# First Fourier layer as 32x32 matmuls over one 32-row operand, with transfer queues in program order

## The chip, the cores and the metric

The kernel runs on one NeuronCore of one Trainium2 chip. The core has a matrix engine (TensorE, PE in the profile; its weight loads are listed apart as PEld), a vector engine (VectorE, DVE), a scalar engine (ScalarE, ACT), GpSimd (POOL) and SyncE (SP). Here SP and POOL do hardly anything but issue transfers. All transfers share the core's 16 DMA engines. Matmul results go to PSUM, an accumulator memory that DVE and ACT read out. The metric is the device time of one execution in microseconds (us); lower is better. All arithmetic is in fp32, and every fp32 matmul appears in the profile as two instructions (two passes), each with its own weight load.

## The reference, cut to what matters

Eight images of 8 channels and 256x256 pixels pass through two blocks. The first, `conv_preact`, is a small Fourier neural operator with a residual; the second is a 3x3 dilation with a residual.

```python
x = x + L0(_gn(x))        # _gn: normalised over 2 channels per group
x = x + L1(_gn(x))        # L1: maximum over a 3x3 window, border -2

def L0(x):                # G = 4 groups, 2 channels each
    h = gconv1x1(concat(x, grid_row, grid_col), fc0_w, fc0_b)   # 10 channels per group
    for i in range(4):
        h1 = spectral_conv(h, sp_w1[i], sp_w2[i])  # rfft2, 12 + 12 rows x 12 columns, irfft2
        h2 = gconv1x1(h, w_w[i], w_b[i])
        h = h1 + h2
        if i < 3: h = gswish(h, betas[i])          # h * sigmoid(softplus(beta) * h) / 1.1
    h = gswish(gconv1x1(h, fc1_w, fc1_b), betas[3])   # 10 -> 128 per group
    return gconv1x1(h, fc2_w, fc2_b)                  # 128 -> 2 per group
```

The change concerns the first pass of the loop (i = 0, "layer 0" below). There h is a linear map of x and of the pixel's coordinates, and both versions take h2 from x directly, with fc0 and w_w multiplied into one matrix.

## The kernel before, in words

**State.** The hidden state of one image lies in one SBUF tile `h`, 128 partitions by 11 chunks (`NCH`) by 4 by 512. Each block of 32 partitions holds 3 row blocks of 10 channels (30 rows used), and the two inner dimensions hold pairs of image rows, so that a chunk carries at most 24 rows of every channel.

**A layer.** For each layer `l` of 0 to 3, `spectrum_h` and `mix` (for layer 0 `spectrum_x` and `mix`, from the image itself) make the layer's output spectrum on PE and DVE. Their result is `fz`, 32 rows by 10 channels by 4 groups by 32 columns; column 24 holds a constant term and column 25 a term linear in the pixel's column. `rows_of` turns the column transform of `fz` into the tile `zt` with matmuls (L397 or L402). Then `layer` walks over the 11 chunks:

- `burst(c)` (L442) forms the chunk's new state in two PSUM tiles. First come 16 matmuls for the 1x1 convolution: K=32, M=32, N=512 from `h` (L452) in layers 1 to 3, and K=6, M=32, N=512 from `x` (L449) in layer 0, where `h` holds only 6 rows of `x` in each block. Then 8 matmuls, K=32, M=128, N=256, add the row transform `zt` times the table `binv` of waves (L455). ACT reads the two PSUM tiles back into `h` with the activation (L461, or L463 in layer 3).
- `turn(c-1)` transposes the previous chunk (16 matmuls, L424; two copies out by L194), and `transform(c-2)` takes its forward transform (L437, copy L438). Both are for the next layer, and layer 3 has neither.
- In layer 3 `stored[c]` (L465) writes the chunk to DRAM from SP.

**The head.** `head(b)` is a generator of 128 steps over the stored state of image b: `load_state` (L580, 256 KB on SP), `first` (8 matmuls L588, two activations L590) and, every second step, `second` (16 matmuls L610, a DVE add L615 into the tile `y`, which was loaded from `x` at L603). It runs inside the layers of image b+1. The generators yield costs, and the main loop (L705 to L718) hands out head steps between the chunks: in layers 0 to 2 two, one, one steps per chunk (`CHUNK`), in layer 3 two per chunk (`LAST`). `dilate(b)` runs behind the head, a piece after each such step, with its loads and stores on POOL (L646, L674).

**The next image's start.** `start(b+1)` loads spectral weights (`load_sw`, L342, 400 KB) and the image (`load_x`, L73, two times 1 MB, on SP), takes statistics on DVE (L227, L199) and small PE matmuls (L202, L210), and goes on to the spectrum and `mix`. It is handed out as side work of layer 3: `room += SIDE` (4.2) per chunk, less what each piece yields. By these costs the load belongs to chunk 0, the first four L227 to chunk 1, L202 and L210 to chunk 3, and the load of the third spectral weight (L360) to chunk 9, after that chunk's `stored`.

**Order.** All PSUM tiles of 2 banks share one tag with 4 buffers (`ps_z`, L57). The main loop stands in `tc.manual_schedule(engines={PE, DVE, ACT})`: those three run in the order written, and the framework's scheduler chooses the order of the instructions on SP and POOL. For layer 0 all 44 loads of `x` rows (`read_x`, L467, 48 KB each) are written ahead of the chunk loop; the rows can be overwritten once `stored[c]` of the image before has been read out.

Of the kernel before, what the change touches and what calls it, by code (L numbers as in the profile page):

```python
# [10 lines left out]
F32 = mybir.dt.float32  # L11
# [9 lines left out]
G = 4  # L21
# [19 lines left out]
LAST = (2,)  # L41
SIDE = 4.2
# [3 lines left out]
def fno_dilate_kernel(ctx: ExitStack, tc: tile.TileContext, a: dict, out: bass.AP):  # L46
    nc = tc.nc
    mm = nc.tensor.matmul
    PE, DVE, ACT = mybir.EngineType.PE, mybir.EngineType.DVE, mybir.EngineType.Activation
# [41 lines left out]
    wt = load("wt", (128, 4, G, 32))  # L91
    eh0 = load("eh0", (128, 3, 2, 32), nc.sync)
# [14 lines left out]
    h = const.tile([128, NCH, NQ, PIX], F32, tag="h", name="h")  # L107
    yin = const.tile([128, DR + 2, HW + 2], F32, tag="yin", name="yin")
# [12 lines left out]
    def softplus(t, n, name):  # L121
        e = const.tile([128, n], F32, tag=f"{name}_e", name=f"{name}_e")
# [5 lines left out]
        sp = const.tile([128, n], F32, tag=f"{name}_sp", name=f"{name}_sp")  # L128
# [3 lines left out]
        rs = const.tile([128, n], F32, tag=f"{name}_rs", name=f"{name}_rs")  # L132
# [6 lines left out]
    sp_p, rs_p = softplus(beta_p, 4, "bp")  # L139
    sp_a, rs_a = softplus(beta_a, 4 * G, "ba")  # L140
# [9 lines left out]
    wc = const.tile([128, 32], F32, tag="wc", name="wc")  # L150
# [13 lines left out]
    cv = const.tile([3, WID, G], F32, tag="cv", name="cv")  # L164
# [180 lines left out]
    def mix(b, l, out_):  # L345
# [28 lines left out]
        if l == 0:  # L374
# [6 lines left out]
                p[0:1, 240 : 240 + WID * G].rearrange("p (o g) -> p o g", o=WID), ALU.add)  # L381
        if l < 2:
            nc.vector.tensor_copy(fz[0:32, :, :, 25], cz[:, 4 if l == 0 else 3])
# [31 lines left out]

    def layer(b, l, out_, stored, side):
# [25 lines left out]
        def burst(c):  # L442
            pair = [ps_z(f"p_z_{b}_{l}_{c}_{i}") for i in range(2)]
            for f in range(NQ):
                for q in range(NQ):
                    o = pair[q // 2][part(f), q % 2, :]
                    if l == 0:
                        k = slice(32 * q, 32 * q + 6)
                        mm(o, wcn[k, :], h[k, c, f, :], start=True, stop=False)  # L449
                    else:  # L450
                        g = f if group_in_f else q
                        mm(o, wt[part(q), l, g, :], h[part(q), c, f, :], start=True, stop=False)  # L452
            for s in range(2):
                for q in range(NQ):
                    mm(pair[q // 2][:, q % 2, HW * s : HW * (s + 1)],  # L455
                       zt[part(q), 2 * c + s].rearrange("p f o -> p (f o)"), binv[part(q), :],
                       start=False, stop=s == 1)
# [9 lines left out]
        def read_x(c):  # L467
            for g in range(G):
                nc.sync.dma_start(
                    h[32 * g : 32 * g + 6, c].rearrange("p f w -> p (f w)"), a["xp"][b, c, g])  # L470

        if l == 0:
            for c in range(NCH):
                read_x(c)
            wcn = sb.tile([128, 32], F32, tag="wcn", bufs=1, name=f"wcn_{b}")
            nc.vector.tensor_scalar(wcn, wc, out_["mr"][:, 1:2], None, ALU.mult)
        room = 0.0
        yield ()
        for c in range(NCH):
            burst(c)  # L480
# [24 lines left out]
    def layers(b, stored, d, then):  # L505

        for l in range(4):  # L510
            if l > 0:
                yield from spectrum_h(b, l, d)
                yield from mix(b, l, d)
            yield from rows_of(b, l)
            yield from layer(b, l, d, stored, then if l == 3 else iter(()))
        yield from then


    spare = h.rearrange("p c f w -> p (c f w)")
# [48 lines left out]
    def head(b, stored, stats):  # L568
        hs, acts, box = {}, {}, {}
# [5 lines left out]
        def load_state(k):  # L575

            if k < NQ * NCH:
                j, c = k // NCH, k % NCH
# [301 lines left out]
```

## Time and profile before

| | us |
|---|---|
| median of 3 runs (4303.44 to 4309.84) | 4309.13 |
| the profiled execution, its own time | 4309.43 |
| its span, first to last instruction | 4307.7 |

| engine | busy us | share of the span | instructions |
|---|---|---|---|
| PE | 4089.1 | 95% | 52330 |
| PEld | 1925.6 | 45% | 52330 |
| ACT | 2772.9 | 64% | 2886 |
| DVE | 2297.3 | 53% | 3424 |
| POOL | 117.0 | 3% | 202 |

The mean granted PE clock is 0.982. The queues moved 344.65 MB, 80 GB/s over the span. In a timeline a row begins with the start and the duration in us; several instructions of one kind are merged (x16), and square brackets hold the idle time of that engine before it and what released it. Because matmuls are pipelined and their ends modelled, the time that a group of matmuls takes is read from its start to the start of the next group, not from its busy time.

### The profile page before, as it was taken

To read this page: it belongs to the slowest core of one execution; us is meant where nothing else is said; L and a number is where in the kernel's file an instruction comes from. 1 tells how busy PE (TensorE), PEld (TensorE's weight loads), DVE (VectorE), ACT (ScalarE), POOL (GpSimd) and SP (SyncE) were. 2 spreads that over 40 slices of the span, in tenths; PEclk is the share of its full clock that TensorE was granted. 3 is DMA by queue.
4 is the path that set the end of the run, shared out by engine and by line. 5 is a ranking of instruction groups with operands and counts; after the bars stand their busy time and mean duration, and the time that the engine had idled before them with its cause. 6 is when DMAs were issued, how large, how long until landed. Compare 5 with 4: busy or idle time off the path is not lost. (4 is left out here: it accounts for less than half of the span.)

```text
span 4307.7 us, 115455 instructions
## 1 busy us (share of the span) xinstructions
PE 4089.1 (95%) x52330; PEld 1925.6 (45%) x52330; DVE 2297.3 (53%) x3424; ACT 2772.9 (64%) x2886; POOL 117.0 (3%) x202
## 2 busy tenths in 40 slices
PE   5877999999999999999999999999999999999997
PEld 3544454444443444434444354444454444444222
DVE  4444544555655555655556555655655555654433
ACT  3435656766667666576666756667666766567887
POOL 1000000000000000000000000000000000000000
PEclk8988999999999999999999999999999999999999
DMA  2014101332114221242112511134111332114321
GB/s 78 13 40 151 53 28 43 135 103 62 55 53 161 87 62 52 75 171 58 52 59 81 182 42 53 50 104 159 55 45 53 136 120 62 48 57 147 109 60 46
DMA packets 113682, 344.65 MB, mean 80 GB/s; under 512 B 15611, under 2 KB 18107, under 8 KB 97768
## 3 DMA queue, kind: packets, MB, share of 16 engines
q1 hardware_dynamic: 95000, 276.18, 20.3%
q0 software_dynamic: 18192, 61.08, 4.3%
q8 instruction: 411, 6.73, 0.7%
q14 instruction: 79, 0.65, 0.1%
HBM read 213.21 MB, written 123.74 MB: 78 GB/s over the span
## 5 line engine op out<-in xcount | busy, mean ns | idle before, releaser
L590 ACT ACTIVATE act<-p_fc 128x1024 f32<-128x1024 f32 x2048 | 1968.9, 1025 | 1202.4 <-PE p_fc L588 1200.6
L588 PE MATMUL p_fc<-hs,c_w 32*128 32x512 f32 x8192 | 1191.6, 633 | 15.3 <-DVE turned L194 8.6
L610 PE MATMUL p_fc<-act,c_w 128*32 128x512 f32 x8192 | 986.7, 597 | 38.9 <-ACT act L590 25.6
L194 DVE COPY turned<-p_t 128x1024 f32<-128x1024 f32 x495 | 584.6, 1219 | 707.7 <-PE p_t L424 707.0
L588 PEld LDWEIGHTS p_fc<-hs,c_w 32*128 32x128 f32 x8192 | 383.6, 183 | 622.8 <-issue 240.9
L461 ACT ACTIVATE h<-p_z 128x1024 f32<-128x1024 f32 x528 | 512.9, 1023 | 117.4 <-PE p_z L455 116.7
L424 PE MATMUL p_t<-ident,h 128*128 128x128 f32 x4224 | 525.8, 278 | 0.0
L615 DVE TENSOR_TENSOR y<-p_fc,y 128x512 f32<-128x512 f32 x392 | 270.7, 690 | 474.9 <-PE p_fc L610 473.0
L610 PEld LDWEIGHTS p_fc<-act,c_w 128*32 128x32 f32 x8192 | 229.9, 109 | 647.4 <-issue 333.0
L424 PEld LDWEIGHTS p_t<-ident,h 128*128 128x128 f32 x4224 | 463.3, 142 | 98.5 <-ACT act L590 64.7
L455 PE MATMUL p_z<-c_binv,zt 32*128 32x256 f32 x5632 | 408.6, 404 | 1.0 <-ACT zt L192 1.0
L455 PEld LDWEIGHTS p_z<-c_binv,zt 32*128 32x128 f32 x5632 | 258.3, 185 | 304.4 <-issue 292.7
L452 PE MATMUL p_z<-h,c_wt 32*32 32x512 f32 x8448 | 317.0, 601 | 0.0
L437 PE MATMUL p_d<-turned,c_fw 128*32 128x240 f32 x4224 | 268.1, 371 | 4.1 <-ACT act L590 2.1
L194 DVE COPY zt<-p_g 128x264 f32<-128x264 f32 x300 | 159.0, 626 | 139.8 <-PE p_g L397 75.0
L463 ACT ACTIVATE h<-p_z,c_bias 128x1024 f32<-128x1024 f32 x176 | 186.6, 1111 | 26.4 <-PE p_z L455 25.9
L355 DVE TENSOR_REDUCE S<-turned 128x80 f32<-128x800 f32 x192 | 188.8, 983 | 5.0
L352 DVE TENSOR_TENSOR turned<-t,B 128x800 f32<-128x800 f32 x192 | 188.4, 981 | 0.5 <-DMA t<-in_spw 0.4
L452 PEld LDWEIGHTS p_z<-h,c_wt 32*32 32x32 f32 x8448 | 72.3, 103 | 190.1 <-ACT act L590 85.7
L437 PEld LDWEIGHTS p_d<-turned,c_fw 128*32 128x32 f32 x4224 | 109.6, 108 | 100.4 <-issue 39.1
L194 DVE COPY turned<-p_at 88x1024 f32<-88x1024 f32 x90 | 101.7, 1155 | 73.8 <-PE p_at L313 73.8
L438 DVE COPY zt<-p_d 128x240 f32<-128x240 f32 x264 | 105.5, 400 | 51.1 <-PE p_d L437 51.1
(170 smaller groups left out, 2023.8 us busy)
## 6 DMA issues: line engine op xcount, KB each, us to landing
stored<-h SPq DMA_DIRECT2D x88, 1024.0 KB
hs<-stored SPq DMA_DIRECT2D x352, 256.0 KB
t<-in_spw SPq DMA_DIRECT2D x96, 400.0 KB
yin<-y_rows POOLq DMA_DIRECT2D x56, 512.0 KB, 4.7
h<-in_xp SPq DMA_DIRECT2D x352, 48.0 KB
turned<-in_x SPq DMA_DIRECT2D x16, 1024.0 KB
y<-in_x SPq DMA_DIRECT2D x56, 256.0 KB
y_rows<-y POOLq DMA_DIRECT2D x56, 256.0 KB, 2.4
```

The source lines that it names most:

```text
L194: nc.vector.tensor_copy(dst, src)
L352: nc.vector.tensor_tensor(pr, sw[k], bt[:, k2, k].unsqueeze(2).to_broadcast([128, G, 2 * WID, WID]), ALU.mult)
L355: nc.vector.tensor_reduce(s[k2][:, k].rearrange("p g s o -> p (g s o)"), pr.rearrange("p g m i -> p (g m) i"), AX.X, ALU.add,)
L424: nc.tensor.transpose(t[:, i // 4, 128 * (i % 4) : 128 * (i % 4 + 1)], h[:, c, i // 2, 256 * (i % 2) + 128 * v : 256 * (i % 2) + 128 * (v ...
L437: mm(p[part(g), :240], fw[:, v, :], m[:, :, :, : NBLK * WID], start=v == 0, stop=v == 1)
L452: mm(o, wt[part(q), l, g, :], h[part(q), c, f, :], start=True, stop=False)
L455: mm(pair[q // 2][:, q % 2, HW * s : HW * (s + 1)], zt[part(q), 2 * c + s].rearrange("p f o -> p (f o)"), binv[part(q), :], start=False, s ...
L461: nc.scalar.activation(dst, pair[i], AF.Silu)
L588: mm(pair[g // 2][:, g % 2, :], w1[part(g), blk, :], hs[k][part(g), :], start=True, stop=True)
L590: nc.scalar.activation(act[:, 2 * i : 2 * i + 2, :], pair[i], AF.Silu)
L610: mm(acc[part(g), :], w2[:, g, 15 - rb - i : 47 - rb - i], act[:, g, :], start=i == 0, stop=i == 1)
L615: nc.vector.tensor_tensor(y, sums, y, ALU.add)
```

## The change

- **Layer 0 in one pass.** `h[:, c]` now gets 32 full rows in each block before its burst: 26 rows of waves (the rows of `binv`, from a new table `wave`, 208 KB per block, issued from POOL) and the 6 rows of `x` (48 KB per block, from SP as before). The weights for `x` go into columns 26 to 31 of `fz`: a small product per image (`wsel` times the constant `wk`, 4 matmuls, K=32, M=32, N=60, in two further PSUM tiles, and two DVE copies), written into `mix` behind the add at L379. `rowg` selects them, so that `rows_of` carries them into `zt`. `burst` in layer 0 is then 32 matmuls, K=32, M=32, N=256, with nothing accumulated across matmuls, in place of 16 + 8. `wcn` is gone. Layers 1 to 3 keep their burst; the added rows meet zero rows of `binv` there.
- **Reads of x and waves.** The first 4 chunks (`AHEAD`) are read ahead of `rows_of`, the others 4 chunks ahead inside the loop.
- **Queues.** SP and POOL join the manual schedule: their instructions run in the order written.
- **Head.** The first two `load_state` of the new image's head are written ahead of the last burst of layer 3; the load of `y` is written 12 steps ahead of its first use.
- **Room.** The small set-up tiles (`softplus`, `wc`, `cv`) lie in an unused part of `h`.

```diff
+AHEAD = 4
...
+    ws = spare[:, 22472:22482]
+    nc.vector.tensor_tensor(ws, wc[:, 0:WID], wc[:, WID : 2 * WID], ALU.add)
+    nc.vector.tensor_tensor(ws, ws, wc[:, 2 * WID : 3 * WID], ALU.add)
+    wk = const.tile([128, WID, 6], F32, tag="wk", name="wk")
+    nc.vector.tensor_tensor(
+        wk, ws.unsqueeze(2).to_broadcast([128, WID, 6]),
+        xrow[:, 0:6].unsqueeze(1).to_broadcast([128, WID, 6]), ALU.mult)
...
+            wsel = sb.tile([128, 32], F32, tag="wsel", bufs=1, name=f"wsel_{b}")
+            nc.vector.tensor_scalar(wsel, xrow[:, 6:38], mr[:, 1:2], None, ALU.mult)
+            pair = [ps_z(f"p_wk_{b}_{i}") for i in range(2)]
+            for g in range(G):
+                mm(pair[g // 2][0:32, g % 2, : 6 * WID], wsel[part(g), :],
+                   wk[part(g)].rearrange("p o i -> p (o i)"), start=True, stop=True)
+            for i in range(2):
+                nc.vector.tensor_copy(
+                    fz[0:32, :, 2 * i : 2 * i + 2, 26:32].rearrange("p o g i -> p g o i"),
+                    pair[i][0:32, :, : 6 * WID].rearrange("p g (o i) -> p g o i", o=WID))
...
+    def read_x(b, c):
+        for g in range(G):
+            nc.gpsimd.dma_start(
+                h[32 * g : 32 * g + 26, c].rearrange("p f w -> p (f w)"), a["wave"])
+            nc.sync.dma_start(
+                h[32 * g + 26 : 32 * g + 32, c].rearrange("p f w -> p (f w)"), a["xp"][b, c, g])
...
-            for f in range(NQ):
-                for q in range(NQ):
-                    o = pair[q // 2][part(f), q % 2, :]
-                    if l == 0:
-                        k = slice(32 * q, 32 * q + 6)
-                        mm(o, wcn[k, :], h[k, c, f, :], start=True, stop=False)
...
+            if l == 0:
+                for s in range(2):
+                    cols = slice(HW * s, HW * (s + 1))
+                    for f in range(NQ):
+                        for q in range(NQ):
+                            mm(pair[q // 2][part(f), q % 2, cols], zt[part(q), 2 * c + s, f, :],
+                               h[part(q), c, f, cols], start=True, stop=True)
...
-        if l == 0:
-            for c in range(NCH):
-                read_x(c)
-            wcn = sb.tile([128, 32], F32, tag="wcn", bufs=1, name=f"wcn_{b}")
-            nc.vector.tensor_scalar(wcn, wc, out_["mr"][:, 1:2], None, ALU.mult)
...
         for c in range(NCH):
+            if l == 0 and c + AHEAD < NCH:
+                read_x(b, c + AHEAD)
+            if l == 3 and c == NCH - 1:
+                for k in range(2):
+                    out_["pieces"][1](k)
             burst(c)
...
+            if l == 0:
+                for c in range(AHEAD):
+                    read_x(b, c)
             yield from rows_of(b, l)
...
-        load_state(0)
-        load_state(1)
+        load_y(0)
         for n in range(STEPS):
+            if n % 16 == 8 and n // 16 < 7:
+                load_y(n // 16 + 1)
...
-    with tc.manual_schedule(engines={PE, DVE, ACT}):
+    with tc.manual_schedule(engines={E.PE, E.DVE, E.Activation, E.SP, E.Pool}):
```

## The prediction

> **What bounds the kernel now.** I read the page first: span, busy rows, slices.
>
> ```profile
> span 4307.7 us, 115455 instructions
> PE 4089.1 (95%) x52330; PEld 1925.6 (45%) x52330; DVE 2297.3 (53%) x3424; ACT 2772.9 (64%) x2886; POOL 117.0 (3%) x202
> ...
> PE   5877999999999999999999999999999999999997
> ```
>
> PE is busy in every slice but those of the first image. In the list of waits, PE's matmuls wait for no transfer after the start. So time is lost or won where PE's order of work gets shorter or has to wait. Next, the timeline of one layer-0 chunk with head work (image 3):
>
> ```profile
> 2013.71 1.14 PE L588 MATMUL p_fc<-hs,c_w 32*128 32x512 f32 x8
> 2014.79 1.18 PE L449 MATMUL p_z<-h,wcn 6*32 6x512 f32 x32
> 2014.95 1.94 ACT L590 ACTIVATE act<-p_fc 128x1024 f32<-128x1024 f32 x2 [2.03 <-PE p_fc L588]
> 2015.90 1.15 PE L455 MATMUL p_z<-c_binv,zt 32*128 32x256 f32 x16
> 2016.97 1.73 PEld L424 LDWEIGHTS p_t<-ident,h 128*128 128x128 f32 x16 [0.33 <-ACT act L590]
> 2016.97 1.97 PE L424 MATMUL p_t<-ident,h 128*128 128x128 f32 x16
> 2017.08 1.95 ACT L461 ACTIVATE h<-p_z 128x1024 f32<-128x1024 f32 x2 [0.19 <-PE p_z L455]
> 2018.87 1.02 PE L437 MATMUL p_d<-turned,c_fw 128*32 128x240 f32 x16
> 2019.71 1.90 PE L610 MATMUL p_fc<-act,c_w 128*32 128x512 f32 x16
> ```
>
> From start to start the burst takes 1.11 (L449) + 1.07 (L455) = 2.18 us, turn 1.90, transform 0.84 to 0.95, a `first` 1.07, a `second` 1.85; PE never pauses. ACT idles 2.03 us ahead of its pair, so it isn't the bound here yet.
>
> Last, the moved transfers: SP, DVE and PE where layer 3 of image 2 begins, three answers of the timeline.
>
> ```profile
> 1815.44 1.87 SPq L73 DMA_DIRECT2D turned<-in_x  x2
> ...
> 1855.76 0.32 SPq L465 DMA_DIRECT2D stored<-h  x1
> ...
> 1918.01 0.35 SPq L342 DMA_DIRECT2D t<-in_spw  x1
> ...
> 1926.77 0.35 SPq L465 DMA_DIRECT2D stored<-h  x1
> ```
>
> ```profile
> 1857.38 2.46 DVE L227 BATCH_NORM_STATS2 bn_x<-turned 128x6 f32<-128x512 f32 x4
> ...
> 1867.40 0.37 DVE L199 BATCH_NORM_AGGREGATE mv_x<-bn_x 128x2 f32<-128x48 f32 x1
> ...
> 1927.63 0.98 DVE L352 TENSOR_TENSOR turned<-t,B 128x800 f32<-128x800 f32 x1
> ```
>
> ```profile
> 1872.71 0.38 PE L202 MATMUL p_st_x<-mv_x,c_grp 128*128 128x1 f32 x2
> 1873.88 0.35 PE L210 MATMUL p_sv_x<-mv_x,c_grp 128*128 128x1 f32 x2 [0.79 <-DVE mv_x L207]
> ```
>
> The scheduler issues the next image's load 42 us before the statistics that read it, and the third spectral weight 9.6 us before its use. The code writes the load behind `stored[0]` (1855.76), and the weight behind `stored[9]` (1926.77).
>
> **The burst.** It loses 32 + 16 instructions and gets 64. L449 runs sixteen tiles at a time: 32 instructions are two passes of 512 columns, 1.11 us. L455 runs four at a time: four passes of 256, 1.07 us. The new burst is sixteen at a time and four passes of 256 columns, the same columns as either: I take 1.10. Below, 64 loads and matmuls of L279 take 0.98 us (367.56 to 368.54); above, 96 of L325 take 3.65 (2056.28 to 2059.93), 2.43 for 64, longer than now. L449 and L455 are nearer: same tiles, same operands.
>
> With head work the shorter burst doesn't count in full. `ps_z` has four buffers; turn takes the pair of the preceding `first`, and the next `first` starts with the burst's second. From the end of a `first` ACT needs 0.16 + 1.94 + 1.94 + 0.10 for release = 4.14 us for four activations, while PE needs burst + 1.90 + 0.94. Below 1.30 us of burst, ACT decides. So 2.18 - 1.30 = 0.88 in each of chunks 1 to 10; chunk 0 (two steps, no turn) has six activations in about 6.1 us against 6.46 measured: 0.4. That is 9.2 per image, 64 for seven. Image 0 has no head, and PE stays the bound (1.10 + 1.90 + 0.95 against three ACT operations, 2.96): 11 x 1.06 = 12. **Gain: 76 us.**
>
> [...] The 2.03 us that ACT idles above show that the limit isn't reached today; no run here has crossed it.
>
> **The image load.** SP in written order issues `stored[0]` when ACT is done, then two weights, then the image. All share the engines, which move 393 GB/s here (window 1857 to 1858). 256 KB from POOL land in 2.3 us, so about 1.65 of it is fixed. 1 MB takes 2.67 us, a weight 1.04: the first half lands at 1855.76 + 1.65 + 2.67 + 2.08 + 2.67 = 1864.8. The statistics wait 7.4 us on DVE. Behind them stand L655, L657, the add of `second`, L659, the other four L227, L199, L662 to L673 and L204 to L207, on whose result PE's L210 waits. Adding their durations puts L207's end at 78.1 against 73.7, as DVE's idle pieces (1.8, 0.5 and 1.0 us) are used up. PE and ACT have no slack: 4.5 us, for six images 27. Bounds: 0, if the delay is worked off, and 7.4. Between images 0 and 1 nothing fills the wait: `stored[0]` at 340.95 gives both halves by 352.7, L199 by 355 where it ended at 342, and L202 (345.43) waits 9.5.
>
> **The third spectral weight.** Issued behind `stored[9]`: 1926.77 + 1.65 + 2.67 + 1.04 = 1932.1, where L352 starts at 1927.63. 4.5 late, less 1.87 of idle DVE ahead of the add at 1933.42: the fold matmuls L371 start 2.6 late, six times: 16, and 2 after image 0. Bounds 0 and 4.5 each.
>
> **The product for x.** `wsel` stands behind L379 (0.21), is an operation like L476 (0.21) and frees PE at 1936.1, where `first` now starts at 1935.56. 8 matmuls at L371's rate (32 in 0.95) with start-up are 0.35, and the next `first` needs one of the new PSUM tiles, read by a copy of about 0.4 (between 0.18 for 32x40 and 0.58 for 32x240): 1.4 us, six times, 8.4. At image 0's start and after it, all of it with both copies lies open: 2 x 1.7. Set-up adds three DVE operations, 0.7. 12.5 in all. Bounds: 0.8 each (no PSUM wait), and 4.3 if `first` gets p_f's buffer, which four copies (2.42) read until later.
>
> **At no cost.** 352 wave loads at 0.54 (the row of y_rows stores) are 190 us on POOL, which is busy for 117; what queues behind them are `dilate`'s loads and stores, with two steps (some 10 us) to land. Per chunk of 6.8 us 1.07 MB arrive, 157 GB/s, with four chunks of lead, under DMA that reaches 393. Without that lead, each chunk's 2.7 us of transfer would show: 8 x 11 x 2.7 = 240. The 352 loads of x move on SP from layer 3 to behind the stores. The head's 256 KB loads stay six steps ahead (20 us and more); `y` goes from 2 to 12 steps. They gain nothing, since PE waits for neither today. Removing L476 frees 0.21 of DVE.
>
> **Clock.** A window in which PE starves after image 0 shows half clock:
>
> ```profile
> 380.00:385.00 5.00, 0.30 (x8) 0.34 (x12) 4.49 (x8) 0.00 (x0) 0.00 (x0) 0.63 0.88 369
> 385.00:390.00 5.00, 2.29 (x35) 1.68 (x28) 1.32 (x4) 1.71 (x3) 0.00 (x0) 0.50 0.39 90
> ```
>
> (PEclk is the third number from the end.) The new pause of 9.5 us should bring as much again, those of 4.5 little: 3 us, from 0 to 12. [...]
>
> **Sum.** 4309.4 (the profiled execution, within 0.3 of the median 4309.13) - 76 + 36.5 + 18 + 12.5 + 3 = 4303.4. Runs differ by 0.15%, so 0.2% (8.6 us) is what can be told from no change: I forecast a little faster, within that.
>
> **Rivals.** (1) The late loads don't show, because the written order isn't what holds SP back, or because DVE works the delay off; for it, DVE is busy for only half. 4303.4 - 36.5 - 18 - 3 = 4246; half of it, 4275. (2) Slower: the 64 weight loads of a burst don't stay ahead of passes of only 0.21 us. Price: a load (0.10) and a start of sixteen (0.1) in each of four passes, a burst near 1.77: the gain falls to 36, 4343. For it speaks L325's rate; against it, that L449 hides its loads. It decides from a burst of 1.49, where the gain is 61. (3) `first` after the product gets p_f's buffer: 2.9 more in seven places, 4324. (4) The change does what it says, but wave reads come late at each layer's start, 5 us per image: 4343; POOL can issue them early, which speaks against it.
>
> **How the numbers follow.** The walked case 0.45 (own range 4285 to 4320: 0.18 faster, 0.19 same, 0.08 slower), rival 1 0.20, rival 2 0.15, rivals 3 and 4 together 0.20 (0.19 slower, 0.01 same). Faster 0.38, same 0.20, slower 0.42. The range takes most of rival 1 and the prices of the others: 4258 to 4343.
>
> **What would show it.** Right: in layer 0 bursts of about 1.1 us from first matmul to L424, with about 0.2 of waits for ACT around them; ACT's idle time ahead of L590 there near nothing; a DVE wait of about 7 us at L227 and one of 4 at L352 in layer 3, both released by transfers, and L210 and L371 late. Wrong: bursts above 1.5; DVE waits on transfers under 2 us; PE waiting for `h` to land.

## The result, and the profile after

| | us |
|---|---|
| before, median of 4 runs (4303.44 to 4309.84) | 4306.52 |
| after, median of 4 runs (4399.21 to 4407.72) | 4403.67 |
| ratio, 95% interval | 1.0225 (1.0207 to 1.0243) |
| the profiled execution after, its own time / its span | 4407.72 / 4405.9 |

The kernel is 97 us slower; the forecast was 6 us faster, with a range that ended at 4343. Line numbers have moved: L588, L590, L610 and L615 of the head are L633, L635, L646 and L651; turn is L454, the burst of layers 1 to 3 L485 and L489, the new burst of layer 0 L480; the image's statistics L238, the spectral weights' product L363, the fold L382, the product for x L398.

The page of the kernel after: span, busy rows, PE in 40 slices, and the granted clock in tenths.

```profile
span 4405.9 us, 119404 instructions
...
PE 4077.8 (93%) x53802; PEld 1933.7 (44%) x53802; DVE 2303.4 (52%) x3443; ACT 2766.4 (63%) x2886; POOL 296.7 (7%) x555
...
PE   4875999999999999989999899998999989999997
...
PEclk8987999999999999999999999999999999999998
```

PE is busy for 11 us less than before in a span that is 98 us longer: its work became shorter, and it waits for more than was saved. PE's row has four eights in its later part, each in a slice with layer 3 of an image. The mean clock fell from 0.982 to 0.969: by span x (1 - clock), with more digits of the clock, 138 us of full speed are missing instead of 76.

Where it waits is told by a table that is worked out from the two traces: the moments at which ACT first reads each burst of the first and last chunk of every layer. "Way to" is from the last burst of one layer to the first of the next.

| stretch, all 8 images | before | after | difference |
|---|---|---|---|
| start to the first burst of image 0 | 72.7 | 80.9 | +8.2 |
| layer 0, first to last burst | 594.3 | 553.8 | -40.4 |
| way to layers 1 and 2 | 952.6 | 946.7 | -5.9 |
| layers 1 and 2 | 1139.3 | 1139.4 | +0.1 |
| way to layer 3 | 493.1 | 504.7 | +11.6 |
| layer 3 | 561.5 | 638.0 | +76.6 |
| way to layer 0 of image 1 | 26.8 | 39.5 | +12.7 |
| way to layer 0 of images 2 to 7 | 152.2 | 185.8 | +33.6 |
| behind the last burst | 315.3 | 317.1 | +1.8 |

So 46 us were won, 40 of them within layer 0, and 145 lost elsewhere. Images are counted from 0 here; the prediction's rows "of image 2" at layer 3 and "image 3" at layer 0 belong to layer 3 of image 3 and layer 0 of image 4 in this count. First the gain: the timeline of a chunk in layer 0 of image 4 with head work of image 3, which answers to the one shown of before.

```profile
2061.17 1.14 PE L633 MATMUL p_fc<-hs,c_w 32*128 32x512 f32 x8
...
2062.24 1.01 PEld L480 LDWEIGHTS p_z<-h,zt 32*32 32x32 f32 x64 [0.76 <-DVE y L651]
2062.24 1.49 PE L480 MATMUL p_z<-h,zt 32*32 32x256 f32 x64
...
2062.40 1.94 ACT L635 ACTIVATE act<-p_fc 128x1024 f32<-128x1024 f32 x2 [3.28 <-PE p_fc L633]
...
2063.66 1.96 PE L454 MATMUL p_t<-ident,h 128*128 128x128 f32 x16
...
2064.23 1.95 ACT L495 ACTIVATE h<-p_z 128x1024 f32<-128x1024 f32 x2
```

From its start to the turn behind it the burst takes 1.42 us (the median over 80 bursts is 1.43), not 1.10. Three steady chunks take 20.66 us where they took 22.95, so 0.76 per chunk; in image 0, without a head, 12.81 against 15.02. Over the 80 steps from burst to burst that the table counts this makes 61 us, and the table shows 40. The first chunks of layer 0 lose the rest. Image 1 takes 0.4 us longer than before: 6.8 us of its layer 0 run at half clock and PE pauses for 2.9 us, where before it was 0 and 0.3. Images 2 to 7 gain 5.6 us each on average instead of 7.6.

Now the loss in layer 3: SP's timeline where layer 3 of image 3 begins, and DVE and PE behind it.

```profile
1905.14 0.32 SPq L499 DMA_DIRECT2D stored<-h  x1
1905.52 1.39 SPq L353 DMA_DIRECT2D t<-in_spw  x2
1906.96 1.53 SPq L74 DMA_DIRECT2D turned<-in_x  x2
```

```profile
1913.54 1.05 PE L485 MATMUL p_z<-h,c_wt 32*32 32x512 f32 x4
...
1914.59 2.47 DVE L238 BATCH_NORM_STATS2 bn_x<-turned 128x6 f32<-128x512 f32 x4 [7.74 <-DMA turned<-in_x]
1916.98 0.34 DVE L692 TENSOR_SCALAR yin<-yin,c_edge 128x258 f32<-128x258 f32 x1
1917.35 1.23 DVE L694 TENSOR_TENSOR m<-yin 128x1024 f32<-128x1024 f32 x1
1918.49 0.68 DVE L651 TENSOR_TENSOR y<-p_fc,y 128x512 f32<-128x512 f32 x1
...
1919.23 2.01 PE L485 MATMUL p_z<-h,c_wt 32*32 32x512 f32 x28 [4.65 <-DVE y L651]
...
1921.17 2.09 PE L489 MATMUL p_z<-c_binv,zt 32*128 32x256 f32 x16
```

The image is issued behind `stored[0]`, 1.8 us after it, and DVE stands 7.74 us at its statistics. PE stops in the very next burst, after 4 of its 32 instructions: the second PSUM tile of the burst is the one that `second` had written, and the add that reads it out (L651) stands on DVE behind the statistics. In the kernel before, the same add (L615) was done 0.3 us ahead of the same burst; a row of DVE and two of PE:

```profile
1863.17 0.69 DVE L615 TENSOR_TENSOR y<-p_fc,y 128x512 f32<-128x512 f32 x1 [1.81 <-PE p_fc L610]
```

```profile
1864.15 1.14 PE L452 MATMUL p_z<-h,c_wt 32*32 32x512 f32 x32
1865.22 1.16 PE L455 MATMUL p_z<-c_binv,zt 32*128 32x256 f32 x16
```

After the pause the clock falls (windows; PEclk is the third number from the end):

```profile
1914.00:1918.00 4.00, 0.58 (x4) 0.00 (x0) 3.38 (x6) 1.59 (x2) 0.00 (x0) 1.00 1.01 375
1918.00:1925.00 7.00, 5.77 (x56) 2.30 (x60) 6.30 (x10) 1.71 (x2) 0.00 (x0) 0.51 0.37 150
1925.00:1929.00 4.00, 4.00 (x60) 0.97 (x59) 2.01 (x6) 3.26 (x5) 0.00 (x0) 1.00 0.72 254
```

The pause of 4.65 us is followed by 6.8 us at half speed: in the clock's records from 1918.1, 1.2 us ahead of the pause's end, to 1924.9. The second pause is at the fold, on the way to layer 0:

```profile
1990.59 0.99 DVE L363 TENSOR_TENSOR turned<-t,B 128x800 f32<-128x800 f32 x1 [4.04 <-DMA t<-in_spw]
```

```profile
1995.46 1.02 PE L382 MATMUL p_f<-F,c_fold 32*32 32x120 f32 x32 [2.14 <-DVE F L374]
...
1997.18 0.42 PE L398 MATMUL p_wk<-wk,wsel 32*32 32x60 f32 x8 [0.54 <-DVE wsel L395]
...
1997.53 2.49 PE L633 MATMUL p_fc<-hs,c_w 32*128 32x512 f32 x8
...
1999.96 3.61 PE L646 MATMUL p_fc<-act,c_w 128*32 128x512 f32 x16
...
2003.49 1.14 PE L633 MATMUL p_fc<-hs,c_w 32*128 32x512 f32 x8
```

DVE waits 4.04 us for the third spectral weight, the fold comes 2.1 us late, and the `first` and `second` behind it take twice their time. Here 2.14 us of idle PE, with the small matmuls of the fold and the product around them, were followed by half clock. Behind this fold and three others among images 2 to 7 the half clock lasts 6.8 us, behind the other two 3.4 us, though the pauses there (3.1 us) are longer than this one.

### The profile page after: what moved, and what is told of

Same layout as the page of the kernel before. It is cut to its first block, busy times and chain, and to the rows that moved or that the text cites. A ratio compares the mean times of both kernels' runs of the same rounds, so it can differ in the third digit from the quotient of the medians.

```text
span 4405.9 us, 119404 instructions
## 1 busy us (share of the span) xinstructions
PE 4077.8 (93%) x53802; PEld 1933.7 (44%) x53802; DVE 2303.4 (52%) x3443; ACT 2766.4 (63%) x2886; POOL 296.7 (7%) x555
## 5 line engine op out<-in xcount | busy, mean ns | idle before, releaser
L635 ACT ACTIVATE act<-p_fc 128x1024 f32<-128x1024 f32 x2048 | 1969.0, 1024 | 1225.7 <-PE p_fc L633 1224.0
L633 PE MATMUL p_fc<-hs,c_w 32*128 32x512 f32 x8192 | 1208.8, 639 | 16.6 <-DVE turned L205 8.5
L646 PE MATMUL p_fc<-act,c_w 128*32 128x512 f32 x8192 | 994.1, 601 | 35.3 <-ACT act L635 25.8
L633 PEld LDWEIGHTS p_fc<-hs,c_w 32*128 32x128 f32 x8192 | 390.9, 185 | 631.6 <-issue 232.8
L454 PE MATMUL p_t<-ident,h 128*128 128x128 f32 x4224 | 525.7, 278 | 2.9 <-issue 2.7
L651 DVE TENSOR_TENSOR y<-p_fc,y 128x512 f32<-128x512 f32 x392 | 270.6, 690 | 491.6 <-PE p_fc L646 490.3
L646 PEld LDWEIGHTS p_fc<-act,c_w 128*32 128x32 f32 x8192 | 231.7, 110 | 654.7 <-issue 339.4
L454 PEld LDWEIGHTS p_t<-ident,h 128*128 128x128 f32 x4224 | 462.4, 142 | 108.9 <-ACT act L635 70.2
L485 PE MATMUL p_z<-h,c_wt 32*32 32x512 f32 x8448 | 332.3, 612 | 29.5 <-DVE y L651 27.0
L489 PE MATMUL p_z<-c_binv,zt 32*128 32x256 f32 x4224 | 313.2, 409 | 6.0 <-issue 5.4
L489 PEld LDWEIGHTS p_z<-c_binv,zt 32*128 32x128 f32 x4224 | 197.5, 189 | 242.1 <-issue 232.7
L441 POOL DMA_DIRECT2D h<-in_wave x352 | 178.4, 509 | 550.2 <-DMA stored<-h 290.9
L363 DVE TENSOR_TENSOR turned<-t,B 128x800 f32<-128x800 f32 x192 | 188.5, 982 | 48.9 <-DMA t<-in_spw 48.8
L485 PEld LDWEIGHTS p_z<-h,c_wt 32*32 32x32 f32 x8448 | 73.8, 103 | 226.7 <-ACT act L635 81.2
L659 POOL DMA_DIRECT2D y_rows<-y x56 | 30.5, 545 | 1957.8 <-DVE y L651 1861.4
L480 PE MATMUL p_z<-h,zt 32*32 32x256 f32 x5632 | 147.6, 393 | 12.0 <-ACT act L635 8.9
```

Source lines behind the costliest of these rows:

```text
L363: nc.vector.tensor_tensor(pr, sw[k], bt[:, k2, k].unsqueeze(2).to_broadcast([128, G, 2 * WID, WID]), ALU.mult)
L454: nc.tensor.transpose(t[:, i // 4, 128 * (i % 4) : 128 * (i % 4 + 1)], h[:, c, i // 2, 256 * (i % 2) + 128 * v : 256 * (i % 2) + 128 * (v ...
L485: mm(pair[q // 2][part(f), q % 2, :], wt[part(q), l, f if group_in_f else q, :], h[part(q), c, f, :], start=True, stop=False)
L489: mm(pair[q // 2][:, q % 2, HW * s : HW * (s + 1)], zt[part(q), 2 * c + s].rearrange("p f o -> p (f o)"), binv[part(q), :], start=False, s ...
L633: mm(pair[g // 2][:, g % 2, :], w1[part(g), blk, :], hs[k][part(g), :], start=True, stop=True)
L635: nc.scalar.activation(act[:, 2 * i : 2 * i + 2, :], pair[i], AF.Silu)
```

## The experiments

All times are medians, beside those of the kernel before on the same chip. e1, e3, e10 and e12 are edits of the changed kernel, e2 of the one before; e5 builds on e1; e4, e6, e7, e8 and e11 on e3; e9 and e13 on e8; e14 on e13 and e15 on e14.

| experiment | time | before | ratio |
|---|---|---|---|
| e1 free queues | 4391.5 | 4306.8 | 1.0195 |
| e2 before, in order | 4474.0 | 4306.8 | 1.0388 |
| e3 early loads | 4302.6 | 4306.8 | 0.9992 (0.9983 to 1.0001) |
| e4 early product | 4320.7 | 4306.8 | 1.0026 |
| e5 free, three weights | 4409.0 | 4307.3 | 1.0240 |
| e6 early, three weights | 4310.5 | 4307.3 | 1.0012 |
| e7 half the loads | 4268.3 | 4307.3 | 0.9911 |
| e8 product behind scaling | 4297.7 | 4307.3 | 0.9980 (0.9971 to 0.9989) |
| e9 free POOL | 4297.4 | 4306.6 | 0.9979 (0.9969 to 0.9988) |
| e10 only the image early | 4341.2 | 4306.6 | 1.0086 |
| e11 old burst | 4329.3 | 4306.6 | 1.0054 |
| e12 only the third weight | 4363.5 | 4306.6 | 1.0134 |
| e13 waves from SP | 4316.2 | 4307.1 | 1.0021 |
| e14 state loads a step later | 4303.0 | 4307.1 | 0.9990 (0.9980 to 1.0000) |
| e15 first y early | 4255.9 | 4306.4 | 0.9881 (0.9865 to 0.9898) |

**Is it the written order of the queues?** Theory A says that transfers are issued late by SP's written order; theory B that the added work costs. The first experiment takes the order of SP and POOL away from the changed kernel, the second gives it to the kernel before.

```diff
-    with tc.manual_schedule(engines={E.PE, E.DVE, E.Activation, E.SP, E.Pool}):
+    with tc.manual_schedule(engines={E.PE, E.DVE, E.Activation}):
```

> The changed kernel, but only PE, DVE and ACT keep the written order; SP and POOL are ordered by the framework again. Theory A (the time went into transfers that SP's written order issues late, and into the half clock that each pause draws): layer 3 of images 0 to 6, first to last burst, goes back from 55.6 and 82 to 91 us to 38 and 77; the waits of DVE for the image (65.8 us in 8 waits) and for the third spectral weight (48.8 us) fall under 10 us each; half clock after 420 us falls from 131 to under 75 us. Time 4285 to 4315, against 4403.7. Theory B (the time went into the work that was added: 75 MB of wave reads and the product for x): above 4380 whatever the order.

```diff
-    with tc.manual_schedule(engines={PE, DVE, ACT}):
+    with tc.manual_schedule(engines={PE, DVE, ACT, mybir.EngineType.SP, mybir.EngineType.Pool}):
```

> The kernel before, with SP and POOL in written order as well, and nothing else of the change. Theory A: the late image and the late weight appear in it too: layer 3 near 55 us in image 0 and 82 to 91 us in the others, together 75 us; some 13 to 25 us more on the way to layer 0. Time 4380 to 4410, as slow as the changed kernel or slower than it by the burst's gain less the product's cost. Theory B: within 15 us of 4306.5.

The list of waits of e1, then of e2 (engine, line, what it waited for: us in total, times, longest):

```profile
DVE turned L363 <- DMA t<-in_spw: 130.7, 8, 19.1
```

```profile
DVE y L613 <- DMA y<-in_x: 134.0, 8, 19.1
DVE bn_x L227 <- DMA turned<-in_x: 65.9, 8, 14.1
...
DVE turned L352 <- DMA t<-in_spw: 27.2, 7, 4.3
```

In e1 layer 3 did return to its old length (2.6 us longer in all than before, against 76.6 in the kernel after), but the time hardly moved: now the framework issues the third weight behind reads of x that wait for `stored`, and the way to layer 0 is 116 us longer in images 2 to 7. So the expectation of e1 failed by 76 us, though its layer-3 half was met. In e2 the kernel before gets the same wait for the image (65.9 us against 65.8 after), without any of the added work, and loses 69 us in layer 3; beyond the expected range it also waits 134 us for `y`, which it issues only two head steps ahead. Theory A holds for layer 3; that any free order would do is refuted.

**Only the place of the issues.** e3 keeps the written order on all five engines and moves three issues in the text.

```diff
                 yield from spectrum_h(b, l, d)
+                if l == 3 and b + 1 < n_img:
+                    load_x(b + 1)
                 yield from mix(b, l, d)
+                if l == 3 and b + 1 < n_img:
+                    ahead["sw"] = [load_sw(0, 0), load_sw(0, 1)]
...
-            if l == 3:
-                nc.sync.dma_start(stored[c], ...)      # in burst(c)
...
                 room -= next(side, SIDE)
+            if l == 3:
+                nc.sync.dma_start(stored[c], ...)
```

> The changed kernel in written order on all five engines, with three issues moved in the text: the next image's load to behind the spectrum of layer 3, its first two spectral weights to behind the mix of layer 3, and stored[c] to behind the side work of its chunk (so that the third weight is issued ahead of it). Theory A: what is lost is the place, not the written order as such: layer 3 at 38 and 77 us, no wait of DVE for the image or for the weights over 2 us, time 4285 to 4315, as with free queues within 10 us. Theory B: above 4380.

It gives back 101 us, as expected, though not every wait is gone: three of DVE for the third weight stay, 18.3 us together. Layer 3 is 8 us longer than before in place of 77, the way to layer 0 of images 2 to 7 3.9 in place of 33.6. The prices of the two loads apart:

> The changed kernel with one issue moved: the next image's load to behind the spectrum of layer 3. The weights and stored[c] stay where the change has them. Theory A: layer 3 goes back to within 2 us per image of before (76.6 us less), the way to layer 0 stays 3 to 6 us long per image for the late third weight and the half clock behind it: 4318 to 4338, against 4403.7. If the late third weight was the larger part: above 4350.

> The changed kernel with one issue moved: stored[9] to behind the side work of its chunk, so that the third spectral weight is issued ahead of it. Theory A: DVE's wait for that weight goes (4 to 5 us per image), and with it PE's pause of 2.3 to 3.2 at the fold and the half clock behind it (3 us), 5 to 6 us in each of six images, while layer 3's 76.6 us for the image stay: 4365 to 4385, against 4403.7. If the half clock at the product has another cause: 4388 to 4404.

e10 (only `load_x` moved) wins 62.5 us, e12 (only `stored[9]` behind its side work) 40.2; together 102.7, about what e3 wins. In e10 layer 3 loses 12 us instead of 77; its time is 3 us above the range. In e12 the way to layer 0 is 0.6 us longer per image than before, in place of 5.6: with the weight in time the half clock behind the fold is gone too, which shows that the product did not cause it. Its time is 1.5 us below the range; 9 of the 40 us come on the way to image 1.

**One weight less to place.** e5 gives e1 a third weight buffer, so that all three weights load together; e6 does the same to e3. Room for it came from the head's states (three buffers, not four) and the dilation's result (one, not two).

```diff
-        t = sb.tile([128, G, 2 * WID, WID], F32, tag="sw")
+        t = sb.tile([128, G, 2 * WID, WID], F32, tag="sw", bufs=3)
...
-            out_["sw"] = [load_sw(0, 0), load_sw(0, 1)]
+            out_["sw"] = [load_sw(0, k) for k in range(3)]
```

> Free queues as in the first experiment, and three buffers instead of two for the spectral weights, so that the third is loaded together with the first two and waits for no buffer (room for it: three buffers instead of four for the head's states, one instead of two for the dilation's result). Theory A (with free queues the whole loss is the third weight, which the framework issues behind reads of x that wait for stored rows: 130.7 us of DVE waits in 8 places, 116 us on the way to layer 0 in images 2 to 7): that way falls back to within 2 us per image of before, half clock after 420 us from 150 to under 60 us, time 4262 to 4285. If something else holds DVE there: above 4370.

The list of waits of e5:

```profile
PE p_fc L631 <- DMA hs<-stored: 113.5, 24, 10.5
```

The weight's waits are gone, and the way to layer 0 is as long as in e1 (123 us more than before in images 2 to 7): in the free order it is now the head's states that come late. What SP holds up is whatever stands behind a read of x that waits for `stored`; in e5's timeline SP spends 12.02 us on five such reads in a row, and 10.60 on three. The third state buffer that was given up may have a part in it; this was not separated.

> Written order with early loads, and the same three buffers. Theory A: the three waits for the weight that were left (18.3 us together, 10.1 the longest, on the way from image 0 to 1) go: time 4285 to 4298, against 4302.6 with early loads alone. If the pause there has another cause: 4300 to 4306.

e6 lost 8 us against e3 instead of winning: the weight's waits went, and 50.8 us of waits for `y` came. It is confounded in the same way, and nothing is concluded from it.

**The burst by itself.**

```diff
-                for s in range(2):
-                    cols = slice(HW * s, HW * (s + 1))
-                    ...  mm(pair[q // 2][part(f), q % 2, cols], zt[part(q), 2 * c + s, f, :], h[part(q), c, f, cols])
+                ...  mm(pair[q // 2][part(f), q % 2, :], zt[part(q), 2 * c, f, :], h[part(q), c, f, :])
```

> Early loads, with the first layer's burst as 16 matmuls of K=32, M=32, N=512 in place of 32 of N=256: the same 1024 columns per PE tile in 32 weight loads instead of 64. It leaves out the second half's own row weights: both halves of a chunk take the first half's, so that the image rows come out wrong; the work beside the loads is the same. Theory A (a burst takes 1.43 us instead of 1.10 because 64 loads do not hide behind passes of 256 columns): the burst takes 1.07 to 1.12. The time then tells the limit by ACT that the prediction set at a burst of 1.30: with it 4285 to 4293, without it (PE goes on being the bound) 4270 to 4280, against 4302.6. If the passes themselves are slow: a burst of 1.3 to 1.45, time within 5 us of 4302.6.

The timeline of e7 in a chunk with head work:

```profile
2004.00 1.18 PE L476 MATMUL p_z<-h,zt 32*32 32x512 f32 x32
...
2004.16 1.94 ACT L635 ACTIVATE act<-p_fc 128x1024 f32<-128x1024 f32 x2 [3.15 <-PE p_fc L633]
2005.23 1.78 PEld L452 LDWEIGHTS p_t<-ident,h 128*128 128x128 f32 x16 [0.97 <-ACT act L635]
```

In image 0, without a head, three chunks take 11.80 us: 15.02 - 11.80 = 3 x 1.07, a burst of 1.11. So the 0.3 us go with the 32 further loads and matmul instructions, which e7 takes away together. The trace of the kernel after tells them apart. In the burst at 2062.24 the passes of 256 columns follow each other by 0.21 to 0.24 us, but the third, begun at 2062.70, stands for 0.19 us after its first instruction: 30 of the 32 weight loads for the second half of the columns start only from 2062.885 on, and the matmuls of that pass then start 4 to 5 ns behind their loads. So the loads that do not get ahead account for 0.19 of the 0.3 us. With head work the turn waits for ACT (L635) and the burst lasts 1.24; three chunks take 20.24, 0.90 per chunk less than before: as good as a burst of 1.28, where the prediction had set ACT's limit at 1.30. The time, 4268.3, is 17 us below the range that goes with this limit, so the time alone would have spoken for the other reading. The chunks decide: 0.14 us in 77 chunks and 0.34 in 11 are 14.5 of the 34 us; most of the rest is fewer pauses (7.5 us without a semaphore in 6 places against 17.3 in 11, half clock after the first 420 us 35 us against 50).

e11 puts the old first layer into e3: no waves, no product, 16 + 8 matmuls.

> Early loads and written order on five engines, but the first layer as before: 16 + 8 matmuls per burst, 6 rows of x, no waves, no product. It prices the rewrite of the layer by itself, against the 4302.6 with it. From the steady chunks (22.95 us for three before, 20.66 after) the rewrite saves 0.76 in each of 77 chunks and 0.74 in each of 11, 67 us, less 9 for the product and some 20 for the pauses that the larger stream of instructions and transfers brings: 4330 to 4355. If written order with early loads is worth nothing by itself: 4300 to 4320.

4329.3: the rewrite is worth 26.7 us among early loads, of the 67 that its steady chunks save. It also shows that written order with these early loads is not free: without the rewrite it costs 22.7 us against the kernel before, of which layer 0 has 14.8 and the way to layer 3 7.9.

**The product for x.** e4 moves it to just behind the statistics, e8 behind the scaling of x; the edit shown is that of e8.

```diff
         mr = out_["mr"]
         for i in range(2):
             nc.vector.tensor_scalar(x[:, i], x[:, i], mr[:, 0:1], mr[:, 1:2], ALU.subtract, ALU.mult)
+            if i == 0:
+                nc.vector.tensor_scalar(wsel, xrow[:, 6:38], mr[:, 1:2], None, ALU.mult)
             yield 1.4
+        p = ps_a(f"p_wk_{b}")
+        for g in range(G):
+            mm(p[part(g), : 6 * WID], wsel[part(g), :], wk[part(g)]...)
+        ...                                            # four copies into fz
```

> The same as the one with early loads, and the product for x moved from behind L379's add (where the fold's chain has no slack) to just behind the image's statistics in layer 3, in one PSUM bank with four copies. Theory A, with the product's price read from the trace (0.6 of wait, 0.35, and 3.0 at half clock in each of seven places): 15 to 28 us below the one with early loads, 4260 to 4295. If the half clock there has another cause than the product's pause, at most 8 us below.

> Early loads, with the product for x two side pieces later than in the experiment before: wsel behind the scaling of the first half of x, the matmuls behind the second. Theory A (that version lost because PE stood 2.8 us behind statistics, ACT's square root and wsel, and then ran at half clock): no wait of PE at the product over 0.3 us, layer 3 at 76.6 to 78 us, time 4288 to 4300, against 4302.6 with early loads and 4320.7 there. If four copies or the PSUM buffer are what costs: above 4306.

ACT, DVE and PE of e4:

```profile
1888.23 0.20 ACT L223 ACTIVATE mr_x<-mr_x 128x1 f32<-128x1 f32 x1
1888.46 0.17 DVE L225 RECIPROCAL mr_x<-mr_x 128x1 f32<-128x1 f32 x1 [2.03 <-ACT mr_x L223]
1888.66 0.24 DVE L242 TENSOR_SCALAR wsel<-c_xrow,mr_x 128x32 f32<-128x32 f32 x1
...
1888.96 0.42 PE L245 MATMUL p_wk<-wk,wsel 32*32 32x60 f32 x8 [2.73 <-DVE wsel L242]
...
1891.34 3.54 PE L646 MATMUL p_fc<-act,c_w 128*32 128x512 f32 x16
```

e4 made PE wait 2.7 us for the chain over ACT's square root, and half clock followed (the `second` at 1891.34 takes 3.54): 18 us slower, where 15 to 28 faster had been expected. e8 wins 5 us against e3, at the near end of its range, for layer 3 got longer (15.6 us over before, against 8.1 in e3) and not shorter, as the expectation had it.

**What was left.** At the start, 6 to 9 us more than before stayed in every version that issues waves from POOL and has two weight buffers, and 7 to 8.5 on the way to layer 0 of image 1 in e3, e4, e7, e8 and e9; in e8 both are 7.1. In e11, without waves, both are gone. And in e8 PE stood still in 11 places without any semaphore. Here is one such place in the timeline of the kernel after (PE's last number in brackets: idle for 2.06 us, released by nothing that the profile shows):

```profile
3476.90 1.68 PE L424 MATMUL p_g<-c_rowg,fz 128*32 128x66 f32 x98
...
3480.64 0.60 PE L424 MATMUL p_g<-c_rowg,fz 128*32 128x66 f32 x27 [2.06 <-issue]
...
3481.09 3.42 PE L646 MATMUL p_fc<-act,c_w 128*32 128x512 f32 x15
```

In the records of the transfers each such pause has one 16 KB packet of the instruction queue beside it, here from 3478.4 to 3479.3. Pauses of this kind above 0.8 us, but for the first image's start, come to 22 us in 13 places after and 4 us in 3 before. In all 13 PE goes on 1.3 to 1.6 us after the end of such a packet; that PE waited for instructions is inferred from this, for no view names what it waited for. In 12 of the 13, 0.5 to 0.8 MB of other transfers started in the 3 us ahead of the pause. In the thirteenth, in image 0, there were none, and none in the 3 of before: bulk beside the packet is not the only way to such a pause.

> The version with early loads and the product behind the scaling, with POOL alone given back to the framework's order; SP keeps the written one. In that version PE stands still in 11 places, 21 us together, with no semaphore to wait for, each time with a 16 KB packet of instructions in flight and 0.3 to 0.8 MB of other transfers in the 3 us before. Theory C (instruction packets come late behind bulk that POOL issues in written order, the dilation's rows above all, which run ahead of their use): the pauses fall under 8 us, the excess of layer 3 and of the way to it (28.7 us in images 2 to 7) under 12; time 4268 to 4286, against 4297.7. If POOL's order has no part in it: 4292 to 4303. If the waves then come late: PE waits for them, above 4303.

e9 moved nothing (4297.4): the pauses stayed, 20 us in 11 places, so POOL's order is not their cause. In its trace the dilation's rows no longer precede those at the fourth layer's `rows_of`; a state load and a store of 262 KB each still do.

> The version with early loads and the product behind the scaling, with the wave reads issued from SP, in its written order, and not from POOL. They then start behind the third spectral weight and not 24 us (image 0) or 28 us (image 1) ahead of it. Theory B, in part (the added wave reads, issued as early as POOL can, slow down the weight that shares the transfer engines: 12.2 us from issue to landing at the start, 13.6 before image 1): these become under 5 us, the 7.05 and 7.10 us on the way to layer 0 of images 0 and 1 fall under 2 each, and the time to 4280 to 4290, against 4297.7. If the weight is late for another reason: 4294 to 4302. If SP is then the late one (8 issues of 0.35 us per chunk ahead of the head's loads): above 4303.

```diff
     def read_x(b, c):
         for g in range(G):
-            nc.gpsimd.dma_start(
+            nc.sync.dma_start(
                 h[32 * g : 32 * g + 26, c]..., a["wave"])
```

The third weight of image 0, in e8 (waves from POOL) and in e13 (waves from SP):

```profile
48.54 0.34 SPq L361 DMA_DIRECT2D t<-in_spw  x1
...
60.89 0.99 DVE L371 TENSOR_TENSOR turned<-t,B 128x800 f32<-128x800 f32 x1 [7.51 <-DMA t<-in_spw]
```

```profile
47.84 0.34 SPq L361 DMA_DIRECT2D t<-in_spw  x1
...
52.58 0.98 DVE L371 TENSOR_TENSOR turned<-t,B 128x800 f32<-128x800 f32 x1
```

With waves from POOL the 400 KB take 12.3 us to be there; with the waves issued behind them from SP, DVE uses them 4.7 us after the issue and has not waited. The start returned from +7.1 to -0.9 us, the way to image 1 from +7.1 to -0.5. So theory B holds for these 14 us: POOL has nothing that keeps it from issuing the waves 24 us ahead of the weight. How the weight and the waves share the transfer engines, no run here shows. The time still rose to 4316, as the last line of the expectation had it: DVE now waits 103 us for the head's first `y`, behind 32 reads on SP.

> The same with waves from SP, and each of the head's 256 KB state loads issued one head step (about 3 us) later. Theory C (the pauses of PE without a semaphore come where an instruction packet meets bulk): those at the fourth layer's rows_of, 1.6 to 2.4 us in six images with 262 KB of state load and 262 KB of y_rows store in the 3 us before, go or shrink under 1 us; 8 to 12 us less than with waves from SP alone, 4270 to 4280. If the instruction stream itself is too fast there (256 instructions of PE in 2 us): they stay, and the time within 5 us.

```diff
-            if n % 32 % NBLK == 0:
+            if n % 32 % NBLK == 1:
                 load_state(n // 32 * NCH + n % 32 // NBLK + 2)
```

Of 10 such pauses above 0.8 us one is left, in image 0 and without other transfers beside it, and 13 us are won (8 to 12 forecast); the time, 4303.0, lies above the expected range because e13's waits for `y` stay (103 us). The way to layer 3 of images 2 to 7 is 2.3 us longer than before instead of 14.4. At the place shown above, two lines of e14:

```profile
3387.82 1.70 PE L421 MATMUL p_g<-c_rowg,fz 128*32 128x66 f32 x103
...
3390.04 0.59 PE L421 MATMUL p_g<-c_rowg,fz 128*32 128x66 f32 x25 [0.53 <-issue]
```

The store is still there; without the state load beside it the pause is 0.53 us. Which share of the two sizes or of the queue they come from matters was not tried.

> The version with waves from SP and state loads a step later, with one more issue moved: the head's first load of y to ahead of the last burst of layer 3 (but for the last image, whose y shares its place with the state). Theory: late transfers are the whole loss. DVE's 103 us of waits for y go, layer 0 of images 2 to 7 gives its 43 us back (as with waves from POOL), half clock after 420 us falls from 78 to 40 to 50 us; time 4245 to 4262, against 4303.0 and 4307.1 before. If the waves then hold up the next transfer in SP's order, the head's states: PE waits for hs in layer 0, 4270 to 4300.

```diff
                 for k in range(2):
                     out_["pieces"][1](k)
+                if b + 1 < n_img:
+                    out_["pieces"][3](0)               # load_y(0)
```

4255.9, 1.2% below the kernel before and 148 below the change as made, with the same PE work as after but for where the product stands. The page of e15 and all of its waits of 20 us or more for a transfer:

```profile
span 4256.6 us, 119027 instructions
...
PE   5877999999999999999999999999999999999997
```

```profile
POOL yin L689 <- DMA y_rows<-y: 36.0, 7, 6.1
...
DVE m L700 <- DMA yin<-y_rows: 22.9, 9, 4.9
```

Neither is new (16.1 and 15.6 before), and PE's pauses above 0.8 us after the first 420 us come to 26 us, against 22 before. Layer 0 is 53 us shorter than before, layer 3 4 longer. That the loss came from late transfers and the pauses and half clock they draw is shown by this: no work was taken away, only issues and the product for x were moved.

## Why the prediction was wrong, point by point

- **The image load.** The step "Adding their durations puts L207's end at 78.1 against 73.7 ... 4.5 us, for six images 27" failed, and the largest part of the error lies here. DVE's wait was right (7.4 forecast, 7.74 measured). But it was followed only along the statistics to L210. The prediction named the add of `second` among what stands behind the wait on DVE, and did not ask who waits for the PSUM tile that this add frees: the next burst, 9.7 us ahead of L210 in the trace of before (1864.15 and 1873.88). So PE lost 6.5 us in that one burst (7.63 us to the start of L489, where L455 came after 1.07), 1 us of it at half clock, and more at half clock behind it. Layer 3 cost 76.6 us, of which e10 gives 65 back, against 27 + 9.5 forecast.
- **The clock.** "3 us, from 0 to 12" was the second error, and it multiplied the others. Half clock rose by 125 us in all (278 against 153 in the clock's records), 62 us of full speed. The ground for 3 us was that pauses of 4.5 us bring little; a pause of 2.1 us brought 6.8 us of half speed.
- **The third weight.** The wait (4.5 forecast, 4.04 in image 3, 4.96 in image 6) and the fold's delay (2.6 forecast, 2.1 to 3.5 measured as PE's wait ahead of it) were right. The term, 16 + 2, was too small for the half clock behind it: e12 puts it at 40.
- **"At no cost".** The step on the waves weighed the mean rate (157 of 393 GB/s; its own sizes, four times 208 and 48 KB in 6.8 us, make 154) and POOL's lead, and took running ahead to be harmless. Running ahead was the harm: 14 us in images 0 and 1, by e13. Of the `y` load it said that PE waits for none today, which was true of the free order only: in written order, two steps ahead, it brought 134 us of waits on DVE (e2), so moving it to 12 steps was needed.
- **The burst.** 1.10 forecast, 1.43 measured. The rival of weight loads that lag was right in kind and not in size (1.77); at 1.43 it stays under the 1.49 from which it would decide. The steady gain is 0.76 x 77 + 0.74 x 11 = 67 us against 76, and pauses and half clock at the start of layer 0 and on the way out of it leave 46 of it (40.4 + 5.9 in the table). The 6.46 us "measured" for chunk 0 are in no row: from start to start of L449 it is 6.43 in image 1 and 6.69 to 6.78 later. The limit by ACT, 1.30, was met at 1.28 in e7.
- **The product for x.** 1.4 us per image forecast; in e3, at full clock, PE waits 0.54 for `wsel`, works 0.34 and the `first` behind takes 0.31 longer: 1.2. Right.
- **Not in the prediction:** the pauses beside instruction packets, 18 us more than before, and the half clock behind some; on the way to layer 3, where 6 of the 13 lie, they make 11.3 us, and that way is 11.6 us longer than before.
- **The whole.** The kind of loss was named, and the written order was given as its cause; the terms of the two late loads were too small by a factor of about 2 (36.5 against 76.6, 18 against 40), and the range added no two rivals together. Of the 104 us by which the profiled run (4407.7) misses the sum (4303.4), 40 lie in layer 3, 30 in the gain of layer 0, 18 on the ways to layer 0, 12 on the way to layer 3 and 8 at both ends, less the 3 that the sum had set down for the clock (all beyond what was forecast there). The rival in which the late loads do not show, 4246, is what e15 came near to (4255.9).

## What to carry to other kernels

When a wait moves onto an engine's queue, list all that stands behind it there, and for each operation that reads a PSUM tile out ask which matmul needs that buffer next: that is where the pause came here (4.65 us at L485), not at the end of the chain that the transfer feeds. When a queue goes from the framework's order to the written one, each issue has to be written as early as its buffer allows, behind nothing that waits for late work; and an engine with nothing else to do issues its reads as early as it can, which was too early here for a 400 KB weight on the same transfer engines (12.3 us in e8, under 4.8 in e13). In the kernel after, with PE busy for 93% of the span, the pauses of PE of 2.06 to 5.13 us between 830 and 3600 us cost themselves and 3.4 or 6.8 us at half clock besides.

## What the runs showed of the hardware that was not expected

- Half clock after short pauses: 2.14 us of idle PE at the fold, among small matmuls, were followed by 6.8 us at a clock of 0.50; 4.65 us in layer 3 by the same 6.8. A pause of 2.06 us, to 3480.64, was followed by 3.4 us at 0.50, from 3481.37 on; behind a pause of 2.04 us, to 836.72, the clock stayed at 1.00. What tells the two apart was not shown.
- PE stood still for 0.9 to 2.5 us without a semaphore, 6 of 13 times at `rows_of` of the fourth layer, and went on 1.3 to 1.6 us after the end of a 16 KB instruction packet. Moving the 262 KB state loads by a head step took 9 of 10 such pauses away (e14). That PE wanted for instructions there is inferred.
- A 400 KB load took 12.3 us beside a stream of 208 KB reads issued ahead of it from another queue (e8), and under 4.8 us with these reads issued behind it (e13).
- 64 matmul instructions of 32x32 by 256 columns took 1.43 us, 32 of 512 columns 1.11: in the first, 0.19 us went by before the loads for the second half of the columns started.
